# A tuned transformer kernel whose first two superblocks follow one written order for every engine

## The chip, the cores and the metric

The kernel runs on one core of one Trainium2 chip. The metric is device time in microseconds (us) of one execution. TensorE is called PE here (its weight loads are PEld), VectorE is DVE, ScalarE is ACT, GpSimd is POOL, and SyncE, which issues most of the DMAs, is SP. Each engine executes its own instruction queue strictly in order; engines wait for each other and for DMAs through semaphores.

## The reference

Sixteen sequences of 256 tokens with 256 features pass through a feed-forward block, an attention block and the same feed-forward block again, each with a layernorm in front and a residual around it:

```python
def _L0_ffn_ref(x, W_up, W_gate, W_down):
    def ternary_quant(w):
        scale = jnp.mean(jnp.abs(w)) + EPS          # EPS = 1e-8
        q = jnp.clip(jnp.round(w / scale), -1.0, 1.0) * scale
        return w + jax.lax.stop_gradient(q - w)
    wu, wg, wd = ternary_quant(W_up), ternary_quant(W_gate), ternary_quant(W_down)
    up = jnp.einsum('bsd,ed->bse', x, wu)            # 256 -> 1024
    gate = jnp.einsum('bsd,ed->bse', x, wg)
    hidden = jax.nn.silu(up) * gate
    return jnp.einsum('bse,de->bsd', hidden, wd)     # 1024 -> 256

x = x + 0.5 * _L0_ffn_ref(_layernorm(x), W_up, W_gate, W_down)
x = x + _L0_attn_ref(_layernorm(x), Wq, bq, Wk, bk, Wv, bv)   # 16 heads of 16, 4 key groups, causal
x = x + 0.5 * _L0_ffn_ref(_layernorm(x), W_up, W_gate, W_down)
```

A ternary weight is 0, +scale or -scale: it is not 0 where |w| > scale / 2, and it has the sign of w. The scale is a mean over the whole matrix, so no weight can be used before all of its matrix is loaded and summed.

## The kernel before

**Tiling.** The 4096 tokens are cut into 8 superblocks of 512 tokens (two sequences each). The work on superblock n in pass p (0 for the first feed-forward, 1 for the second) has the key (n, p). A superblock's input stays in a tile `x0` ... `x7`. Each feed-forward is 8 units f = 0 to 7. A unit makes `u` (up) and `g` (gate) by four 512-column matmuls each (two halves of the contraction, and a high and a low f16 part of the normalized input `xT`), then `th` = silu(u) on ACT, `h` = g * th on DVE, and `hT` = the high f16 part of h (a cast on ACT) and the low part (a subtraction on POOL). Four `ffn_down` steps (t = 0 to 3), of 16 matmuls of 256 columns each, make `d` from `hT` and the ternary weights `td`; DVE adds it to x.

**Start.** SP loads x0, the up weights in four pieces, the gate weights, x1, the down weights, the attention weights `wqkv` and the rest of x. The weights are summed (`part_u`, `part_g`, `part_d`), a matmul with ones spreads the sum over the partitions (`allsum_u` and so on), and `ternary_piece` makes the ternary f16 tiles `tu`, `tg`, `td` in pieces of 512 columns: first `dn` = (w < -scale/2), on DVE, ACT or POOL by a letter in `ENG_U`, `ENG_G`, `ENG_D`, then (w > scale/2) - dn on DVE (line 321). Some matmuls of ones with ones (`warm`) stand between the first steps.

**Norms.** x0 and x1 (names `first`, `second`) are normalized and then transposed by PE (`xt`, tile `xT`). Every later norm goes another way: bn_stats and bn_aggr on DVE, `rstd` on POOL (line 339), `shift` and two quarters of `xn` on DVE, two quarters on ACT, the high part of `xparts` on ACT (line 364), the low part on POOL (line 367), and a transposing DMA on SP (line 372) to `xT_f` (feed-forward) or `xT_a` (attention). The first attention projection of superblock n, tile `qkv` (line 525), needs `xT_a` of n, and the scaled attention weights `wparts` (DVE and POOL, lines 1026 and 1027).

**Attention.** After `qkv`, the parts of q and k go through DRAM (`kd`, `qd`) back into `Qs` and `ks`, with constant rows that POOL makes at the start (`constant_rows`, lines 243 to 253) and SP copies there. Tiles `s`, `tops`, `pparts`, `pt` find row maxima; `st`, `pT`, `o`, `oT`, `ot` are scores, exponentials, products with the values and their transposes.

**What sets the order.** A planner, `run`, pops steps from five chains (feed-forward units, loads, maxima, attention, projections) by written costs and lags, and issues their instructions. The scheduling layer under it then orders each engine's queue by its own estimate of times, unless a piece of code asks for its program order. So the order at the start comes from the planner's constants (`C1`, `C2`, `TD`, `DR`, `PM`, `LAG_NORM0` and so on) and from that layer.

```python
    for at, fn in (
        (16, constant_queries), (PM + 11, projections_split), (KM, constant_rows), (KV, constant_values), ...
        (C3, lambda: ternary_columns(3)), (C2, lambda: ternary_columns(2)), (C1, lambda: ternary_columns(1)),
    ):
        f.insert(at, Step(0.0, fn))
    run(f, [prepares(), load_chain(), sequence_chain(), peak_chain(), qkv_chain()])
```

Of the kernel before, what the change touches and what calls it, by code (L numbers as in the profile page):

```python
# [8 lines left out]
F32 = mybir.dt.float32  # L9
F16 = mybir.dt.float16  # L10
# [15 lines left out]
ENG_U = "vvvv"  # L26
ENG_G = "vapa"
ENG_D = "aaaa"
NUF = "000000"
NWF = "404000"  # L30
# [7 lines left out]
NCUT = 4  # L38
PINF = 0
NW4 = 0  # L40
PRE = 0
USUM = 1
GSUM = 0
PING = 0
HPU = 0
GFIRST = 0
PINF1 = 0
TDA = 1
PINK = 1
KM = 2  # L50
KV = 12
PINA = 0
PINM = 1
PINT = 0
NWARM = 12
NWARM2 = 0
NWARM3 = 0
GCUT = 0
# [9 lines left out]
C1 = 1  # L68
C2 = 4
C3 = 5  # L70
TD = 6
DR = 6
DS = 2
PM = 9
LAG_NORM0 = 10.0
DOWN_AT0 = 5
DOWN_GAP0 = 1
GU = 1
# [15 lines left out]
NORM = 1024.0  # L94


@with_exitstack
def macaron_kernel(
# [45 lines left out]

    x_t = x.rearrange("(n s) (t p) e -> n p (s t) e", s=2, t=2)
# [44 lines left out]
    load_x(0)  # L190
    for w, w_t in ((wu, w_upT), (wg, w_gateT)):
        for i in range(NCUT if w is wu or GCUT else 1):
            nn = NCUT if w is wu or GCUT else 1
            cut = slice(i * F // nn, (i + 1) * F // nn)
            nc.sync.dma_start(w[:, :, cut], w_t.rearrange("(c p) f -> p c f", p=P)[:, :, cut])
    load_x(1)
    nc.sync.dma_start(wd, w_downT.rearrange("(c p) e -> p c e", p=P))

    def load_rest():
        nc.sync.dma_start(wqkv, w_qkv.rearrange("(c p) f -> p c f", p=P))  # L200
        nc.sync.dma_start(bqkv, b_qkv)
        for n in range(2, NSB):
            load_x(n)
# [5 lines left out]
    nc.vector.tensor_copy(identh, ident)  # L209
    ones = const.tile([P, P], F32, tag="ones", name="ones")  # L210
    nc.vector.memset(ones, 1.0)
    neg_half = const.tile([P, TT], F32, tag="neg_half", name="neg_half")
    nc.vector.memset(neg_half, -0.5)

    def warm(n, name):
        if n:
            pw = bank([P, P], f"warm_{name}")
            for _ in range(n):
                nc.tensor.matmul(pw, ones, ones, start=True, stop=True)

    warm(NWARM, "start")

# [3 lines left out]

    box = {}
# [10 lines left out]
    def constant_rows():  # L238
# [4 lines left out]
        nc.gpsimd.memset(k[KP:KR], 0.0)  # L243
        ku = k[KP:KR].rearrange("p (v u k) -> p v u k", v=3, k=U)
        for which, base in ((EVEN, 0), (ODD, 32)):
            nc.gpsimd.affine_select(
                out=ku[:, which], in_=ku[:, which], pattern=[[0, S // U], [-1, U]],
                compare_op=ALU.is_ge, fill=-MASK, base=base, channel_multiplier=1,
            )
        nc.gpsimd.memset(k[KR : KR + 3], -MROW)  # L250
        nc.gpsimd.memset(v[KP:KR], 0.0)
        vj = v[KP:KR].rearrange("p (j b) -> p j b", b=4)
        nc.gpsimd.affine_select(
            out=vj, in_=vj, pattern=[[1, 32], [0, 4]], compare_op=ALU.not_equal,
            fill=MASK, base=0, channel_multiplier=-1,
        )
        for to in Ks:
            nc.sync.dma_start(
                to[KP : KR + 3].rearrange("p g v k -> p g (v k)"),
                k[KP : KR + 3].unsqueeze(1).to_broadcast([KR + 3 - KP, G, 3 * S]),  # L260
            )
        box["queries"] = v

    def constant_values():
        for v in VT:
            nc.gpsimd.memset(v, 0.0)
            nc.gpsimd.memset(v[:, :, :, D : D + 1], 1.0)
# [9 lines left out]
    def ternary_sums(w, name):  # L277
        if name == "d":
            cuts = [(w[:, : FC // 2], 1), (w[:, FC // 2 :], 1)]
        elif name == "u" or GCUT:  # L280
            fq = F // NCUT
            cuts = [(w[:, :, i * fq : (i + 1) * fq], 0 if i % 2 == 0 and not USUM else 1) for i in range(NCUT - 1)]
            h = fq // 2
            cuts += [(w[:, :, (NCUT - 1) * fq : (NCUT - 1) * fq + h], 0), (w[:, :, (NCUT - 1) * fq + h :], 1)]
        else:
            cuts = [(w[:, : EC // 2], GSUM), (w[:, EC // 2 :], 1)]
        part = small.tile([P, len(cuts)], F32, tag="part", name=f"part_{name}")
        for i, (piece, on_scalar) in enumerate(cuts):
            if on_scalar:
                junk = fp.tile([P] + list(piece.shape[1:]), F16, tag="th", name=f"junk_{name}_{i}")  # L290
                nc.scalar.activation(junk, piece, AF.Abs, accum_out=part[:, i : i + 1])
            else:
                pin(PING and name == "g", nc.vector.tensor_reduce(
                    part[:, i : i + 1], piece, AX.XY, ALU.add, apply_absolute_value=True
                ))
        return part

    def ternary_scale(w, name, part):
        n = w.shape[1] * w.shape[2]
        allsum = bank([P, part.shape[1]], f"allsum_{name}")  # L300
        nc.tensor.matmul(allsum, ones, part, start=True, stop=True)
        tot = small.tile([P, 1], F32, tag="tot", name=f"tot_{name}")
        nc.vector.tensor_reduce(tot, allsum, AX.X, ALU.add)
        s = const.tile([P, 1], F32, tag=f"s_{name}", name=f"s_{name}")
        nc.vector.tensor_scalar(s, tot, 1.0 / (P * n), TERNARY_EPS, ALU.mult, ALU.add)
        hi = small.tile([P, 1], F32, tag="hi", name=f"hi_{name}")
        nc.vector.tensor_scalar(hi, s, 0.5, None, ALU.mult)
        lo = small.tile([P, 1], F32, tag="lo", name=f"lo_{name}")
        nc.vector.tensor_scalar(lo, s, -0.5, None, ALU.mult)
        return s, hi, lo  # L310

    def ternary_piece(wi, ti, hi, lo, name):
        engine = {"u": ENG_U, "g": ENG_G, "d": ENG_D}[name[0]][int(name[1])]
        dn = fp.tile([P] + list(wi.shape[1:]), BF16, tag="tmp", name=f"dn_{name}")
        if engine == "a":
            nc.scalar.activation(dn, wi, AF.Relu, bias=lo, scale=-1.0)
            nc.scalar.activation(dn, dn, AF.Sign)
        else:
            by = nc.gpsimd if engine == "p" else nc.vector
            pin(PINT and engine == "v", by.tensor_scalar(dn, wi, lo, None, ALU.is_lt))  # L320
        nc.vector.scalar_tensor_tensor(ti, wi, hi, dn, ALU.is_gt, ALU.subtract)  # L321


    def norm_stages(n, name, factor, finish, early=False):
        xn = lnp.tile([P, TT, E], F32, tag="xn", name=f"xn_{name}", bufs=1)
        mv = small.tile([P, TT, nc.vector.BN_AGGR_DIM], F32, tag="mv", name=f"mv_{name}")
        rstd = small.tile([P, TT], F32, tag="rstd", name=f"rstd_{name}")

        def stats():
            st = small.tile([P, TT, nc.vector.BN_STATS_DIM], F32, tag="st", name=f"st_{name}")  # L330
            for t in range(TT):
                pin(PINA if name[0] == "a" else PINF1 if name in ("f0_1", "f0_2") else PINF if name[:2] == "f0" else 0, nc.vector.bn_stats(st[:, t, :], xs[n][:, t, :]))
            for t in range(TT):
                nc.vector.bn_aggr(mv[:, t, :], st[:, t, :])
            ve = small.tile([P, TT], F32, tag="ve", name=f"ve_{name}")
            nc.vector.tensor_scalar(
                ve, mv[:, :, 1], LN_EPS, 1.0 / (factor * factor), ALU.add, ALU.mult
            )
            nc.gpsimd.tensor_tensor(rstd, ve, neg_half, ALU.pow)

        def normalize():
            on_scalar = 2 if name in ("first", "second") else NACT0 if early else NACT
            shift = small.tile([P, TT], F32, tag="shift", name=f"shift_{name}")
            nc.vector.scalar_tensor_tensor(shift, mv[:, :, 0], -1.0, rstd, ALU.mult, ALU.mult)
            for t in range(TT):
                if t < on_scalar:
                    nc.scalar.activation(
                        xn[:, t, :], xs[n][:, t, :], AF.Identity,
                        bias=shift[:, t : t + 1], scale=rstd[:, t : t + 1],
                    )  # L350
                else:
                    nc.vector.tensor_scalar(  # L352
                        xn[:, t, :], xs[n][:, t, :], mv[:, t, 0:1], rstd[:, t : t + 1],
                        ALU.subtract, ALU.mult,
                    )

        return [stats, normalize] + [lambda f=f: f(xn) for f in finish]

    def ffn_norm(n, name, tag="xT", early=False):
        parts = lnp.tile([P, 2, EC, TT, P], F16, tag="xparts", name=f"xparts_{name}")  # L360
        xT = lnp.tile([P, 2 * EC * TT, P], F16, tag=tag, name=f"xT_{name}", bufs=2 if tag == "xT" else 1)

        def high(xn):
            nc.scalar.copy(parts[:, 0].rearrange("p c t e -> p t c e"), xn.rearrange("p t (c e) -> p t c e", c=EC))  # L364

        def low(xn):
            nc.gpsimd.tensor_tensor(  # L367
# [3 lines left out]
            )  # L371
            nc.sync.dma_start(xT, parts.rearrange("p a c t e -> p (a c t e)"), transpose=True)

        view = xT.rearrange("p (a c t) q -> p a c (t q)", a=2, c=EC)
        return view, norm_stages(n, name, NORM, [high, low], early)

    def early_norm(n, name):
# [724 lines left out]
```

## Time and profile before

| | |
|---|---|
| median of 3 runs | 563.08 us (561.78 to 563.2) |
| the profiled execution | 560.4 us; its span 558.7 us |
| PE busy | 537.8 us, 96% of the span |
| DVE, ACT, POOL busy | 433.1, 376.0, 355.0 us (78%, 67%, 64%) |
| TensorE clock granted, mean | 0.991 |

The busy share of PE is an average over stages; matmuls overlap in a pipeline, and a busy PE may run at half clock. The views used below give, for each group of instructions, the start and the duration in us, the engine, the line of the kernel, the operation, the tiles written and read, and in brackets how long that engine had been idle just before and what ended the idleness. SPq is a DMA's issue on SP. In the windows view, a time and a count of instructions stand for each engine, then the granted clock and the DMA engines' share.

### The profile page before, as it was taken

Reading aid. Unit: us, or ns where it says so; the run is one execution under the profiler, and the core shown is the slowest. Engines: PE = TensorE matmul, PEld = TensorE weight load, DVE = VectorE, ACT = ScalarE, POOL = GpSimd, SP = SyncE. Lnnn points to the kernel's source line nnn. Section 1 sums busy time; section 2 is a strip of 40 time slices with the busy share of each in tenths; the row PEclk is TensorE's granted clock in tenths of the full one; section 3 lists DMA queues with packets and bytes.
Section 4 is the critical chain, followed back from the end, with each engine's and each line's share of the span. In section 5 each row is a group of like instructions: output and inputs, shape, how many; then the busy total and the mean of one; then the engine's idle time right before and its main releaser. Section 6 shows DMA issues by size and latency. Waiting matters only on the chain.

```text
span 558.7 us, 12132 instructions
## 1 busy us (share of the span) xinstructions
PE 537.8 (96%) x4593; PEld 330.6 (59%) x4593; DVE 433.1 (78%) x1027; ACT 376.0 (67%) x658; POOL 355.0 (64%) x380
## 2 busy tenths in 40 slices
PE   5999999989999999999999998999999999999997
PEld 5546556647556665665665664566645576565565
DVE  5988989978889899869777887459955697847653
ACT  5796757496688678677766749755698445874642
POOL 4367787675589568577745539854589534865542
PEclk8899999999999999999999999999999999999999
DMA  8933288561077068058249003572024930020201
GB/s 293 299 48 57 39 207 128 161 124 31 12 185 111 1 163 144 4 152 147 27 126 163 1 3 39 144 162 40 1 40 74 207 79 22 12 68 11 67 28 49
DMA packets 119317, 51.25 MB, mean 92 GB/s; under 512 B 85174, under 2 KB 119002, under 8 KB 119258
## 3 DMA queue, kind: packets, MB, share of 16 engines
q1 hardware_dynamic: 118825, 50.08, 40.8%
q8 instruction: 36, 0.59, 0.4%
q10 hardware_dynamic: 432, 0.39, 0.3%
q14 instruction: 24, 0.19, 0.1%
HBM read 22.41 MB, written 14.68 MB: 66 GB/s over the span
## 4 chain that ended last, share of the span: by engine, by line
PE 72%; DVE 11%; ACT 7%; DMA 5%; POOL 3%; issue 2%; SPq 0%; DVEq 0%; ACTq 0%; POOLq 0%
PE d L502 18%; PE u L451 15%; PE g L451 15%; PE o L706 6%; PE s L611 6%; PE st L675 5%; PE qkv L525 4%; DMA Qs<-prows 2%; ACT pT L676 2%; PE ot L722 2%; DVE tops L625 2%; DVE h L486 1%; DVE tmp L485 1%; DMA xT_a<-xparts_a 1%; DVE xn_f L352 1%
## 5 line engine op out<-in xcount | busy, mean ns | idle before, releaser
L492 POOL TENSOR_TENSOR hT<-h,hT 128x512 f16<-128x512 f32 x128 | 149.0, 1169 | 88.0 <-ACT hT L491 87.1
L676 ACT ACTIVATE pT<-st,exp_scale 128x512 f32<-128x512 f32 x192 | 119.8, 697 | 26.3 <-PE st L675 26.2
L502 PE MATMUL d<-td,hT 128*128 128x256 f16 x1024 | 122.5, 273 | 0.2 <-ACT pT L676 0.2
L491 ACT CAST hT<-h 128x512 f16<-128x512 f32 x128 | 79.5, 621 | 56.0 <-DVE h L486 40.9
L625 DVE TENSOR_REDUCE tops<-s 128x8 f32<-128x512 f32 x160 | 103.0, 677 | 16.3 <-PE s L611 15.9
L451 PE MATMUL u<-xT_f,tu 128*128 128x512 f16 x448 | 115.3, 379 | 0.3 <-DVE h L486 0.3
L684 POOL TENSOR_SCALAR_AFFINE_SELECT pT<-pT 128x512 f32<-128x512 f32 x128 | 80.4, 636 | 55.3 <-ACT pT L676 52.9
L451 PE MATMUL g<-xT_f,tg 128*128 128x512 f16 x448 | 115.3, 379 | 0.0
L502 PEld LDWEIGHTS <-hT 128*128 128x128 f16 x1024 | 98.5, 98 | 18.2 <-issue 0.5
L485 DVE SCALAR_TENSOR_TENSOR tmp<-th,u 128x512 f32<-128x512 f32 x96 | 65.5, 683 | 50.4 <-ACT th L483 49.9
L483 ACT ACTIVATE th<-u,half_u 128x512 f32<-128x512 f32 x96 | 66.2, 692 | 42.8 <-PE u L451 42.4
L451 PEld LDWEIGHTS <-tg 128*128 128x128 f16 x512 | 49.9, 98 | 62.0 <-DVE tg L321 2.0
L451 PEld LDWEIGHTS <-tu 128*128 128x128 f16 x512 | 47.2, 99 | 43.1 <-issue 2.0
L486 DVE SCALAR_TENSOR_TENSOR h<-g,tmp 128x512 f32<-128x512 f32 x96 | 65.6, 685 | 5.4
L675 PE MATMUL st<-Qs,ks 99*128 99x512 f16 x192 | 54.1, 380 | 6.3 <-DMA Qs<-prows 3.0
L611 PEld LDWEIGHTS <-Qs 96*128 96x128 f16 x896 | 50.9, 116 | 12.7 <-issue 3.0
L611 PE MATMUL s<-ks,Qs 96*128 96x64 f16 (+2 forms) x896 | 53.4, 208 | 0.0
L706 PE MATMUL o<-pT,vt 128*32 128x128 f32 (+1 forms) x1024 | 49.4, 329 | 0.0
L706 PEld LDWEIGHTS o<-pT,vt 128*32 128x32 f32 x1024 | 28.4, 109 | 25.2 <-issue 8.3
L507 DVE SCALAR_TENSOR_TENSOR x<-d,so,x 128x256 f32<-128x256 f32 x64 | 30.4, 477 | 14.1 <-PE d L502 13.6
L525 PE MATMUL qkv<-xT_a,wparts 128*128 128x512 f16 x144 | 34.6, 379 | 1.9 <-DMA xT_a<-xparts_a 1.9
L367 POOL TENSOR_TENSOR xparts_f<-xn_f,xparts_f 128x1024 f16<-128x1024 f32 x14 | 29.8, 2131 | 10.2 <-ACT xparts_f L364 8.2
(163 smaller groups left out, 603.2 us busy)
## 6 DMA issues: line engine op xcount, KB each, us to landing
qd<-sp SPq DMA_DIRECT2D x32, 256.0 KB, 2.6
Qs<-qd SPq DMA_DIRECT2D x64, 128.0 KB, 3.5
ks<-kd SPq DMA_DIRECT2D x48, 128.0 KB, 3.6
x<-in_x SPq DMA_DIRECT2D x8, 512.0 KB, 8.7
out<-x SPq DMA_DIRECT2D x32, 128.0 KB, 3.1
kd<-sp SPq DMA_DIRECT2D x16, 128.0 KB, 2.4
Qs<-in_w_upT SPq DMA_DIRECT2D x4, 256.0 KB, 5.5
Qs<-in_w_gateT SPq DMA_DIRECT2D x1, 1024.0 KB
```

The source lines that it names most:

```text
L451: nc.tensor.matmul(acc, w[:, c, f * P : (f + 1) * P], ffn_ready[key][:, a, c, :], start=(c == 0 and a == 0), stop=(c == EC - 1 and a == 1),)
L485: nc.vector.scalar_tensor_tensor(tmp, th, 1.0, up, ALU.add, ALU.mult)
L486: nc.vector.scalar_tensor_tensor(h, gate, 0.25 / (NORM * NORM), tmp, ALU.mult, ALU.mult)
L491: nc.scalar.copy(hT[:, f, 0, :], h)
L492: nc.gpsimd.tensor_tensor(hT[:, f, 1, :], h, hT[:, f, 0, :], ALU.subtract)
L502: nc.tensor.matmul(acc, hT[:, f, a, t * P : (t + 1) * P], td[:, f, :], start=(f == 0 and a == 0), stop=(f == FC - 1 and a == 1),)
L611: nc.tensor.matmul(sc[:, at : at + n, :], Qs[0:KR, b // 4, g * P : (g + 1) * P, b % 4], k[:, g, which, first * U : (first + n) * U], start ...
L625: nc.vector.tensor_reduce(peaks[q][:, u, :], sc, AX.X, ALU.max)
L675: nc.tensor.matmul(sc, keys, mov, start=True, stop=True)
L676: nc.scalar.activation(pT[:, u, :].rearrange("p (h b j) -> p h b j", h=4, b=4), sc.rearrange("p (h j b) -> p h b j", h=4, b=4), AF.Exp, sc ...
L684: nc.gpsimd.affine_select(out=v, in_=v, pattern=[[0, 4], [1, P]], compare_op=ALU.is_ge, fill=0.0, base=0, channel_multiplier=-1,)
L706: pin(not first, nc.tensor.matmul(at[:, half * P :], v[:, 2 * s + half, g, :], moving, start=half == 0, stop=half == 1, tile_position=(0, ...
```

## The change

Everything up to the end of superblock (0, 0)'s `ffn_down` and of superblock (1, 0)'s units is taken from the planner and written as one table, `ORDER`, of 191 words; each word issues one small step. Calls go through a wrapper that keeps the program order on each engine while the table is read (`box["in_order"]`). After the table, the planner goes on with superblock (2, 0), with attention, and with the four `ffn_down` of (1, 0); the scheduling layer orders that part as before.

- **Ternary weights:** ACT stores |w| (`sizes`, f32) while it sums it; `sign` = (w >= 0) - 0.5 is made on POOL (`:P`, 8 of 12 pieces of 512 columns) or DVE (`:V`); then one DVE step makes (|w| > cut) * sign. The values are now halves, and the scales carry the factor 2. The sums of up and gate are made in three parts: two on ACT, one of 512 columns on DVE. For the down weights ACT writes |w| in place.
- **Loads:** x0 in two halves by token tiles, up and gate in two halves by rows each, all at the head of SP's queue.
- **Warm matmuls:** 14 at the start, 12 after `all_u`, 4 after `all_g` (before: 12, and two times 4 between the first products).
- **Norms of x0 and x1:** x0 by halves and on DVE alone; x1 as before.
- **Constants of attention:** POOL's memsets of `vt` and its `constant_rows` stand after the table; SP's copies `ks<-constant_rows` follow the first `xT_a` on SP's queue, and the copies `Qs<-constant_rows` stand among the loads of the first two sequences.
- **Planner:** the two table superblocks count as done, and superblock 2's norm as ready.

```diff
-NWARM = 12
+NWARM = 14
+ORDER = """
+st0 ag0 st1 rs0 ag1 xn0 rs1 su0 tr0 xn1 su1 gu1:P su1v tr1 azu gu0:V allu warm12 gu2:V hi00 oneu
+cutu hi01 peru gu3:P tu0a sg0 tu1 sg1v sg1 lo00 gg2:P azg tu0b allg warm4 s1a lo01 gg0:P tu2 U02 tu3
+U04 th02 s1b gg1:P U01 misc th04 agg1 gd3:V U06 th01 cutg gg3:V rs1x tg0b U00 tg0a tg3 G00 gd2:P sh1
+...
+alld U14 th10 cutd miscd td0 H11 U13 rs2 th14 td2 U17 L11 th13 xV2 U16 sh2 h14 xA2 td1 G10 H14 td3
+G17 ph2 L14 h10 D3 th17 pl2 th16 h17 H10 D1 r3 H17 L10 END2 D2 r1 L17 G13 r2 G15 h13 U15 H13 L13 D0
+th15 h15 G16 H15 r0 L15 h16 H16 L16
+"""
...
-    load_x(0)
+    for s in range(2):
+        nc.sync.dma_start(xs[0][:, 2 * s : 2 * s + 2], x_t[0][:, 2 * s : 2 * s + 2])
     for w, w_t in ((wu, w_upT), (wg, w_gateT)):
-        for i in range(NCUT if w is wu or GCUT else 1):
...
+        for c in range(EC):
+            nc.sync.dma_start(w[:, c], w_t[c * P : (c + 1) * P])
...
-        if engine == "a":
-            nc.scalar.activation(dn, wi, AF.Relu, bias=lo, scale=-1.0)
-            nc.scalar.activation(dn, dn, AF.Sign)
-        else:
-            by = nc.gpsimd if engine == "p" else nc.vector
-            pin(PINT and engine == "v", by.tensor_scalar(dn, wi, lo, None, ALU.is_lt))
-        nc.vector.scalar_tensor_tensor(ti, wi, hi, dn, ALU.is_gt, ALU.subtract)
...
+    def size_pass(n, c, lo, hi, i=None):
+        scalar.activation(
+            size[n][:, c, lo:hi], raws[n][:, c, lo:hi], AF.Abs,
+            **({} if i is None else {"accum_out": part[n][:, i : i + 1]}),
+        )
+    def half_sign(engine, n, cut):
+        engine.tensor_scalar(sign[n][cut], raws[n][cut], 0.0, 0.5, ALU.is_ge, ALU.subtract)
+    def ternary(n, cut):
+        src = size[n] if n in size else raws[n]
+        vector.scalar_tensor_tensor(tern[n][cut], src[cut], cuts[n], sign[n][cut], ALU.is_gt, ALU.mult)
...
+    for name in ORDER.split():
+        if name[:4] == "warm":
+            warm(int(name[4:]))
+            continue
+        name, _, engine = name.partition(":")
+        ops[name](*([by[engine]] if engine else []))
+    constant_values()
+    constant_rows()
+    box["in_order"] = False
+    vector.tensor_copy(identh, ident)
+    constant_keys()
...
+    for t in range(TT):
+        issued["down", 0, 0, t] = 0.0
     f = ffn_chain()
-    for at, fn in (
-        (16, constant_queries), (PM + 11, projections_split), (KM, constant_rows), (KV, constant_values), ...
+    for at, fn in ((C_QUERIES, constant_queries), (C_SPLIT, projections_split), (C_TOP, projections_top)):
         f.insert(at, Step(0.0, fn))
```

In the table, U, G, th, h, H, L with two digits are superblock and unit (u, g, silu, join, high, low), D0 to D3 and r0 to r3 are the matmuls and the residual of (0, 0)'s `ffn_down`, g with a letter and a digit is a sign piece and t with them a ternary piece.

The changed kernel, as built, has these orders around the end of the table. PE: D3, D1, D2, then three products, D0, G16, then u and g of (2, 0)'s units 0 to 4 with three `ffn_down` of (1, 0) among them, then `qkv` of superblock 0. DVE after r0's residual: one bn_stats of x0, four of x3, `h`, a small step, five bn_aggr, `h`, a small step, then the variance step of x0. POOL after L16: a `vt` memset, `rstd` of x0, `rstd` of x3, three `hT` low parts with four more memsets among them, the low part of `wparts`, the low part of `xparts_a` of superblock 0. ACT, for the same norm: silu, the first two scalings of `wqkv`, `xn` of x0, the third scaling, an `hT` cast, then the high part of `xparts_a`. SP, after qkv of superblock 0: the transposing DMA of `xT_a` of superblock 1 stands behind 23 DMAs for attention of superblock 0, three of which are the copies `Qs<-constant_rows` (20 DMAs stand there before the change, without these copies).

## The prediction

> **What bounds the kernel now.** I read the page first: PE's busy share and the clock by slices.
>
> ```profile
> PE 537.8 (96%) x4593; PEld 330.6 (59%) x4593; DVE 433.1 (78%) x1027; ACT 376.0 (67%) x658; POOL 355.0 (64%) x380
> ...
> PEclk8899999999999999999999999999999999999999
> ```
>
> PE sets the pace, except in the first slices, where the clock is low too. A gain here must be PE time not lost. So next PE's own timeline of the start, then the granted clock in windows.
>
> ```profile
> 13.69 0.56 PE L301 MATMUL allsum_g<-part_g,ones 128*128 128x2 f32 x2 [0.69 <-ACT xT_first L388]
> 14.11 0.59 PE L451 MATMUL u<-xT_first,tu 128*128 128x512 f16 x1
> ...
> 18.35 1.38 PE L451 MATMUL g<-xT_first,tg 128*128 128x512 f16 x4 [0.67 <-DVE tg L321]
> ...
> 23.49 0.82 PE L451 MATMUL g<-xT_first,tg 128*128 128x512 f16 x3 [0.28 <-DVE tg L321]
> ```
>
> ```profile
> 5.43:8.84 3.41, 0.66 (x6) 0.47 (x5) 1.41 (x9) 2.33 (x7) 1.91 (x3) 1.00 1.01 372
> 8.84:19.08 10.24, 7.35 (x26) 4.90 (x27) 9.37 (x38) 5.62 (x11) 1.01 (x1) 0.50 1.08 353
> ```
>
> DVE is busy 9.37 of 10.24 us; its ternary pieces release PE. PE runs at half clock from 8.84 to 19.08, after 2.75 us of idleness out of 3.41. By 23.49 it has done five groups of four products. A group takes 0.86 us at full clock (the chain of waits steps by 0.86), so PE stands as if it had begun at 23.49 - 5 x 0.86 = 19.2 and never stopped. From there to 43 us it hardly waits.
>
> The table ends near 50 us. So I also read the timeline of the other engines across the first attention norm:
>
> ```profile
> 51.32 0.45 DVE L507 SCALAR_TENSOR_TENSOR x<-d,so,x 128x256 f32<-128x256 f32 x1
> ...
> 52.73 1.01 POOL L339 TENSOR_TENSOR rstd_a<-ve_a,neg_half 128x4 f32<-128x4 f32 x1 [2.90 <-DVE ve_f L336]
> ...
> 54.52 1.08 ACT L347 ACTIVATE xn_a<-x,shift_a,rstd_a 128x256 f32<-128x256 f32 x2
> ...
> 58.50 2.13 POOL L367 TENSOR_TENSOR xparts_a<-xn_a,xparts_a 128x1024 f16<-128x1024 f32 x1
> ...
> 60.66 1.85 SPq L372 DMA_TRANSPOSE xT_a<-xparts_a  x1
> ```
>
> It is 9.3 us from the last residual of superblock 0 to the issue of its transposing DMA. The page gives 4.6 us from issue to landing for xT_f and 5.7 for xT_a. The first qkv starts at 66.27, 5.6 us after the issue, without an idle PE: there is little to spare.
>
> **The start: -4.6 us.** I walk the built queues with these durations. I keep the landing of the weights: ACT reads up's last piece at 8.67 and gate at 11.31. (If longer rows land sooner, the walk gains up to 0.7 us.)
>
> - ACT: two sums of gate are now 1.14 us for 1024 columns and 0.73 for 512 (from the same pass over the old pieces, with the read of the accumulator), so all_g is fed at 12.5, not 13.69.
> - DVE per 512 columns: the last ternary step keeps its 0.66 us start to start. The sign costs the 0.40 of the old dn on 4 pieces and nothing on 8. The sum of a 512-column part is 0.6, against 1.21 for the old gate half.
> - ACT loses the Relu and Sign passes (0.7 + 0.6 us on six pieces) and gains |w| passes of 0.54; it is not late in the walk.
> - POOL: eight sign pieces at 1.73 (the one row, dn_g at 19.78). They end two to four us ahead of their users.
> - 4 warm matmuls (0.21 each at full clock) hide until the last low part of xT; first product at 14.2, fifth group done at 18.9, none waiting more than 0.25 us after that.
>
> So PE stands as if it had begun at 18.9 - 5 x 0.86 = 14.6, against 19.2: -4.6 us.
>
> **POOL's new work: +1.0 (0 to +7).** The dn_g row had no second two-input DVE step on top of it. The hT low parts at 27.48 to 32.7 took 5.26 us for 4, or 1.32, against 1.17 in the page's mean, while DVE made td and tg pieces. If sign pieces took 2.3 us the walk's gate products wait 2.4 us; at 3.0 us, 7. Below nothing is excluded: POOL is early already. I take 1.0, nearer the 1.73 row. The Trainium skill ("SBUF — State Buffer", "SBUF: two separate sides") speaks against this edit: a DVE step with both inputs in SBUF and a GpSimd step that reads SBUF exclude each other for the whole step. Both new steps are of that kind. By that rule alone each sign piece may wait out one 0.75 us ternary step, 2.4 us apiece, and the term would be nearer 2.5.
>
> **The clock: +1.0 (0 to +5).** The row above shows half clock for 10.24 us after 2.75 us idle. The longer warm-up covers the start, but the stall below is 5.5 us idle. Half of 10.24 is 5.1; a dense PE should have it back sooner, and part of it falls into the second stall. The Trainium skill ("TensorE: Matmul & The Clock Gate", "What's actually happening") says one idle window of about 3.4 us halves the clock, and one busy window restores it. By that rule it costs 1.7 us per stall.
>
> **The end of the table: +5.5 (0 to +6.7).** PE, from 18.9: 27 groups of the table (23.3), 8 transposes (0.9), the sum of down (0.4), four downs of 1.75 (7.0), then a transpose and a small matmul (0.4), 10 groups (8.6) and three downs of superblock 1 (5.2): it reaches qkv at 64.7. Now the data:
>
> - D0 ends at 49.5; residual at 49.7. DVE then has five bn_stats (1.7), two h (1.3), five bn_aggr (0.4) and two small steps (0.4) before the variance: 53.9. Before, that step came 1.2 us after the residual; now 4.2.
> - POOL is in L16 until 54.5, then a vt memset (0.46), rstd (1.0): 55.9. DVE's shift and xn: 56.8.
> - ACT has two scalings of wqkv first, which wait for DVE's reciprocal chain (57.0): 57.5 to 58.4. Then xn (1.0), a scaling, a cast, the high part (1.0): 61.2. Before, xn came 0.6 us after shift.
> - POOL has two hT parts, memsets, a third hT part and wparts (2.07, behind DVE's cast at 60.3) first: 63.5. Low part 2.1: 65.6. SP issues at 65.7; landing 4.5 later, 70.2; by the 5.7, 71.4.
>
> PE waits from 64.7 to 70.2. Nothing stands behind qkv in PE's queue that could run: the queue is in order. Before, the same path is 9.3 us; here it is 16, and only 15 us of PE work lie over it after D0.
>
> **The second norm: +3.7 (0 to +4).** From qkv to the next superblock's qkv PE has 20 us of work (5.2 for qkv and values, 14 of products and downs, 0.5 of s): it arrives at 90.2. In before, from the end of that superblock's last down (77.6) to the DMA's issue (87.6) is 10.0 us. Here that down ends at 77.7, the low part at 87.5, and SP reaches the DMA only at 89.4, because three Qs<-constant_rows copies of 0.63 each now stand before it. Landing 93.9.
>
> **The rest: +1.7 (-2 to +5).** The planner goes on from other counts. In before's waits of PE after 110 us: st on prows 3.0, st on pT 2.0, qkv on xT_a 1.9, pt on pparts 1.3, together 8.2. Walking the new queues I find pt (1.7, 2.7), qkv (2.2), st (1.5, 1.8): 9.9. +1.7.
>
> The POOL constants cost nothing on PE otherwise: ks is needed by s 20 us later. The warm matmuls lie in idle time.
>
> **Sum.** -4.6 + 1.0 + 1.0 + 5.5 + 3.7 + 1.7 = +8.3. From the profiled 560.4: 568.7. The median of the runs, 563.08, is 0.5% above that execution; scaled, 571.
>
> **Rivals.**
>
> 1. *Faster:* the first norm's data is there in time. If xT_a of superblock 0 is issued before about 60 us, neither the first wait nor the clock loss exists, and the second shrinks with it: -4.6 + 1.0 + 0.7 = -2.9, or 560. For it: before has no wait there, and the table puts PE early but the norm's chain as early. Against: three queues have been given extra steps ahead of that chain (DVE 3 us, ACT 2, POOL 4). Chance 0.22.
> 2. *The POOL pieces bound the start:* 2.3 to 3.0 us each, gate products waiting; the waits at the table's end stay, since everything moves along: 571 + 1.4 to 6, that is 573 to 577. For it: the 1.32 row; against: POOL's slack of 2 us. Chance 0.18.
> 3. *About nothing:* start and waits cancel; needs the first wait at 2 us and the second at 1. Chance 0.06.
> 4. The forecast, 565 to 573: 0.54.
>
> That the table does not do what it says I leave out: the built queues follow it.
>
> **How the numbers follow.** 0.3% of 563 is 1.7 us, about what a measurement of this kernel can tell from no change. Faster: rival 1. Within: rival 3. Slower: 0.18 + 0.54 = 0.72. The range: 559.5 takes in rival 1's own time and cuts what lies below it (half of its chance), and 577 cuts the top of the POOL bound with a late xT_a.
>
> **What would show it.** PE's first product near 14.2 and the fifth group done near 19; POOL's sign pieces at 1.7 (rival 2: over 2.3, with PE waiting for tg between 18 and 30). PE dense to about 64, then idle 4 to 7 us before qkv, ended by DMA xT_a, and once more, 3 to 4 us, near 90. A PE that runs through both would make the prediction wrong; so would a first product after 17.

## The result, and the profile after

The changed kernel takes 585.26 us (median of 4 runs, 585.13 to 586.83) against 562.46 for the kernel before (the three runs above and one more): the ratio is 1.0421, with a 95% interval of 1.0395 to 1.0448. The forecast was slower, 571; the time is 14 us above it and outside the range of 559.5 to 577.

The page of the changed kernel, PE's busy share, the granted clock by slices, and the group of the attention projections:

```profile
PE 545.2 (93%) x4623; PEld 335.4 (57%) x4623; DVE 443.7 (76%) x1025; ACT 371.0 (64%) x644; POOL 370.2 (63%) x388
...
PEclk9999989599999999899999999999999999999999
...
L139 PE MATMUL qkv<-xT_a,wparts 128*128 128x512 f16 x144 | 38.3, 410 | 18.7 <-DMA xT_a<-xparts_a 18.7
```

All wrapped calls carry the wrapper's line, L139, so one goes by tiles. The slices no longer show a low clock at the start (the windows view still has 0.61 from 10.97 to 15.35), but the eighth slice (102 to 117 us) stands at half clock, and PE waited 18.7 us for `xT_a`. PE's timeline shows where (first three lines: the start, where each f32 matmul shows as two instructions, so x24 are twelve warm matmuls; then both waits):

```profile
10.97 4.55 PE L139 MATMUL warm<-ones 128*128 128x128 f32 x24
15.35 0.74 PE L139 MATMUL all_g<-part_g,ones 128*128 128x1 f32 x6
...
16.92 4.48 PE L139 MATMUL u<-xT_first,tu 128*128 128x512 f16 x20
...
73.96 5.43 PE L139 MATMUL qkv<-xT_a,wparts 128*128 128x512 f16 x18 [5.29 <-DMA xT_a<-xparts_a]
...
97.80 0.64 PE L139 MATMUL s<-ks,Qs 96*128 96x192 f16 x10 [1.61 <-issue]
108.82 2.74 PE L139 MATMUL qkv<-xT_a,wparts 128*128 128x512 f16 x6 [10.37 <-DMA xT_a<-xparts_a]
```

The last `d` before the first wait ends at 68.67 (66.76 plus 1.91). The first product comes at 16.9, not 14.2.

**A ledger of the loss.** Take a matmul's start and subtract the full-speed time of all matmuls ahead of it (the median start-to-start time of each form in all runs). The warm matmuls and those that sum the weights are not counted, since the two kernels have different numbers of them. What is left is the time that PE has lost so far. Read at equal amounts of work, the two profiled executions compare like this:

| PE work done | lost before | lost, changed | difference | what lies in the step |
|---|---|---|---|---|
| 30 us | 18.8 | 16.7 | -2.1 | the start |
| 50 us | 18.9 | 17.8 | -1.1 | `every` waits 0.94 for DVE: +1.0 |
| 60 us | 19.0 | 24.7 | +5.7 | first wait, 5.3, and half clock: +6.8 |
| 70 us | 18.9 | 25.4 | +6.5 | `d` waits 0.55 for `hT`: +0.8 |
| 80 us | 19.2 | 40.5 | +21.3 | second wait, 1.6 + 10.4, and half clock: +14.8 |
| 470 us | 79.3 | 104.2 | +24.9 | the rest: +3.6 |

The spans differ by the same 24.9 (583.6 against 558.7). Three fifths of the loss is the second wait with its half clock. SP's timeline from qkv of superblock 0 to `xT_a` of superblock 1 shows why; first the kernel before (two of its lines), then the changed one:

```profile
69.78 2.21 SPq L372 DMA_TRANSPOSE xT_f<-xparts_f  x1
...
87.61 2.82 SPq L372 DMA_TRANSPOSE xT_a<-xparts_a  x1
```

```profile
74.41 3.15 SPq L249 DMA_DIRECT2D ks<-constant_rows  x3
77.68 5.56 SPq L336 DMA_TRANSPOSE xT_f<-xparts_f  x1
83.33 1.40 SPq L603 DMA_DIRECT2D kd<-sp  x2
84.78 0.65 SPq L261 DMA_DIRECT2D Qs<-constant_rows  x1
...
92.50 6.95 SPq L626 DMA_DIRECT2D Qs<-qd  x8
99.49 0.63 SPq L632 DMA_DIRECT2D ks<-kd  x1
100.16 1.36 SPq L261 DMA_DIRECT2D Qs<-constant_rows  x2
101.63 5.35 SPq L336 DMA_TRANSPOSE xT_a<-xparts_a  x1
```

The second column is how long SP was held by the issue. Behind three `ks` copies the transposing DMA holds SP for 5.56 us instead of 2.21, and everything for attention stands behind it. `xparts_a` of superblock 1 is ready at 96.2 (POOL 94.08 plus 2.14); SP gets to it at 101.63, and its data release PE at 108.8, 7.2 us after the issue. The windows view after the first wait, then around the end of the second (the last three figures are the granted clock, the DMA engines' share and GB/s):

```profile
74.00:76.00 2.00, 2.00 (x5) 0.65 (x5) 0.00 (x0) 0.03 (x1) 1.86 (x3) 0.50 0.00 0
76.00:78.00 2.00, 2.00 (x9) 0.84 (x8) 0.47 (x1) 0.78 (x1) 1.36 (x2) 0.80 0.42 131
...
104.00:108.80 4.80, 0.00 (x0) 0.00 (x0) 0.00 (x0) 0.00 (x0) 0.00 (x0) 0.50 1.14 177
108.80:112.00 3.20, 3.18 (x13) 1.52 (x14) 0.00 (x0) 1.44 (x2) 1.95 (x1) 0.50 0.72 133
112.00:114.50 2.50, 2.50 (x11) 1.08 (x10) 2.00 (x3) 0.38 (x1) 0.57 (x2) 0.53 0.00 0
```

From 104 to 108.8 no engine works and the DMA engines are full. Half clock then costs 1.4 us after the first wait (2 us at 0.50, 2 at 0.80) and 2.8 after the second.

### The profile page after: what moved, and what is told of

Its sections match the earlier page's. It is cut to its first block, busy times and chain, and to the rows that moved or that the text cites. A ratio compares the mean times of both kernels' runs of the same rounds, so it can differ in the third digit from the quotient of the medians.

```text
span 583.6 us, 12183 instructions
## 1 busy us (share of the span) xinstructions
PE 545.2 (93%) x4623; PEld 335.4 (57%) x4623; DVE 443.7 (76%) x1025; ACT 371.0 (64%) x644; POOL 370.2 (63%) x388
## 4 chain that ended last, share of the span: by engine, by line
PE 64%; DVE 14%; DMA 7%; ACT 6%; POOL 5%; issue 2%; SPq 0%; ACTq 0%; DVEq 0%; POOLq 0%
PE d L139 15%; PE u L139 12%; PE g L139 11%; PE o L139 6%; PE s L139 5%; PE qkv L139 5%; PE st L139 5%; DVE h L139 3%; DMA xT_a<-xparts_a 3%; DVE tmp L139 2%; DVE tops L139 2%; PE ot L139 2%; POOL hT L139 2%; ACT pT L139 2%; ACT th L139 2%
## 5 line engine op out<-in xcount | busy, mean ns | idle before, releaser
L139 POOL TENSOR_TENSOR hT<-h,hT 128x512 f16<-128x512 f32 x128 | 149.0, 1169 | 85.3 <-ACT hT L139 84.9
L139 ACT ACTIVATE pT<-st,exp_scale 128x512 f32<-128x512 f32 x192 | 120.6, 694 | 26.0 <-PE st L139 25.8
L139 DVE TENSOR_REDUCE tops<-s 128x8 f32<-128x512 f32 x160 | 103.4, 680 | 27.1 <-PE s L139 27.0
L139 PE MATMUL d<-td,hT 128*128 128x256 f16 x1024 | 122.5, 273 | 0.5 <-POOL hT L139 0.5
L139 ACT CAST hT<-h 128x512 f16<-128x512 f32 x128 | 79.4, 621 | 63.6 <-DVE h L139 63.4
L139 PE MATMUL u<-xT_f,tu 128*128 128x512 f16 x448 | 116.3, 381 | 0.4
L139 POOL TENSOR_SCALAR_AFFINE_SELECT pT<-pT 128x512 f32<-128x512 f32 x128 | 81.0, 637 | 55.8 <-ACT pT L139 55.3
L139 PE MATMUL g<-xT_f,tg 128*128 128x512 f16 x448 | 115.1, 379 | 0.0
L139 PEld LDWEIGHTS <-hT 128*128 128x128 f16 x1024 | 98.9, 98 | 20.4 <-POOL hT L139 0.8
L139 ACT ACTIVATE th<-u,half_u 128x512 f32<-128x512 f32 x96 | 66.1, 690 | 42.2 <-PE u L139 41.4
L139 DVE SCALAR_TENSOR_TENSOR tmp<-th,u 128x512 f32<-128x512 f32 x96 | 65.4, 682 | 35.8 <-ACT th L139 35.2
L139 PEld LDWEIGHTS <-tg 128*128 128x128 f16 x512 | 50.2, 98 | 59.8 <-issue 0.8
L139 PEld LDWEIGHTS <-tu 128*128 128x128 f16 x512 | 47.0, 99 | 44.1 <-issue 2.1
L139 DVE SCALAR_TENSOR_TENSOR h<-g,tmp 128x512 f32<-128x512 f32 x96 | 65.9, 687 | 6.3
L139 PEld LDWEIGHTS <-Qs 96*128 96x128 f16 x896 | 50.7, 117 | 16.8 <-issue 5.8
L139 PE MATMUL s<-ks,Qs 96*128 96x64 f16 (+2 forms) x896 | 53.4, 209 | 3.4 <-issue 1.6
L139 PE MATMUL st<-Qs,ks 99*128 99x512 f16 x192 | 54.0, 380 | 2.4 <-DMA Qs<-prows 1.1
L139 PE MATMUL qkv<-xT_a,wparts 128*128 128x512 f16 x144 | 38.3, 410 | 18.7 <-DMA xT_a<-xparts_a 18.7
L139 PE MATMUL o<-pT,vt 128*32 128x128 f32 (+1 forms) x1024 | 49.1, 329 | 0.2 <-DVE tops L139 0.2
L139 DVE SCALAR_TENSOR_TENSOR x<-d,out_scale,x 128x256 f32<-128x256 f32 x64 | 30.5, 479 | 22.6 <-PE d L139 22.0
L139 POOL TENSOR_TENSOR sp<-full,sp 128x512 f16<-128x512 f32 (+1 forms) x24 | 28.0, 1166 | 22.9 <-DVE sp L139 19.2
L139 PEld LDWEIGHTS o<-pT,vt 128*32 128x32 f32 x1024 | 28.4, 109 | 24.5 <-issue 7.5
```

Of the source, the lines that this page charges most:

```text
L139: ins = fn(*args, **kwargs)
```

## The experiments

The theories are four. A: the constants of attention, late on POOL, SP and the DMA queue, make the waits. B: the norm's own chain on DVE, ACT and POOL is late whatever SP does. C: POOL's work between L16 and `xparts_a` makes the first wait. D, for the start: the loads by halves land late, and idle PE costs the clock (the expectation of experiment 4 has its own letter A for the loads). Time lost always means the ledger. Ratios are to the runs of the kernel before beside them.

**1. The constants not pinned.**

```diff
-    constant_values()
-    constant_rows()
     box["in_order"] = False
+    constant_values()
+    constant_rows()
```

> The changed kernel with one line moved: the program order is switched off before POOL's constants are issued (vt and constant_rows), not after, so the scheduling layer may put them early, and SP's six copies of constant_rows with them, ahead of xT_f of superblock 2. Theory A (the constants late on POOL, SP and the DMA queue make the waits for xT_a): the second wait of PE for xT_a, 12.0 us with the wait before it, falls to 0 to 4, the first, 5.3, to 1 to 5, and the half clock behind them (about 3.5 us) goes with them: 585 falls to 566 to 572. Theory B (the norm's own chain on DVE, ACT and POOL is late, whatever SP does): the first wait stays above 4 and the second above 8, time 579 or more. The start stays as it is in both: first product at 16.9.

580.56 us, ratio 1.0328 (1.0286 to 1.0369). A's number missed; B's number fits, but not its waits. The layer put `xparts_a` ahead of the third `hT` part, and the first wait shrank to 1.2 (for `wparts`) and 1.6 (at `v`). But POOL's `constant_rows` (2.10 us) now lay ahead of `rstd_second`, for which DVE and then PE's `g` waited 0.93 each (18.4 lost at 20 us of work, against 16.4). And the second wait was still 6.3, though no copies of constants stood on SP's queue there any more: PE came to it at 94.1, and `xT_a` was issued at 95.59. So moving these instructions early is not enough by itself: where they go decides, and without the copies the norm of superblock 1 is still late for a PE that comes early.

**2. Only the copies and their source early.**

```diff
-... rs1 su0 tr0 xn1 ...
+... rs1 krow su0 tr0 xn1 ...             # krow: constant_rows, on POOL
     constant_values()                    # the vt memsets stay behind L16
-    constant_rows()
     box["in_order"] = False
     constant_keys()
+    constant_queries()                   # no longer at step C_QUERIES
```

> The changed kernel with constant_rows made at the start of POOL's queue (in the table, behind the second rstd of x0) and SP's six copies issued before xT_f of superblock 2; the vt memsets stay pinned behind L16. Theory A split: if SP and the DMA queue make the second wait, it falls from 12 us to under 3, while the first wait, in which only POOL's memsets could matter, stays at 4 to 6: 571 to 575. If the memsets on POOL make both, the second wait stays over 6: 578 or more. Theory B: 583 or more.

572.29 us, ratio 1.0179 (1.013 to 1.0227). PE's timeline and waits of this run, then SP's two transposing DMAs:

```profile
99.33 1.47 PE L139 MATMUL qkv<-xT_a,wparts 128*128 128x512 f16 x6 [1.08 <-DMA xT_a<-xparts_a]
```

```profile
PE qkv L139 <- DMA xT_a<-xparts_a: 9.3, 3, 5.2
```

```profile
74.90 1.70 SPq L336 DMA_TRANSPOSE xT_f<-xparts_f  x1
...
94.16 3.17 SPq L336 DMA_TRANSPOSE xT_a<-xparts_a  x1
```

The columns of the second, for the whole run, are us in total, times, and the longest. The first wait is 5.2 as before; the second is 1.08, and 26.1 are lost at 80 us of work against 40.5. SP reached `xT_f` at 74.90 for 1.70 us, and `xT_a` at 94.16 instead of 101.63. PE got its data at 99.33, 9.5 us sooner: `xparts_a` was ready 3.2 us earlier (93.0), SP took 1.2 us instead of 5.4 to get to it, and the landing 5.2 instead of 7.2. This shows A for the second wait, worth 13 us of time, and shows that the copies have no part in the first. POOL's steps for `constant_rows` (3.0 us between 69.63 and 77.44 in the changed kernel) moved together with SP's copies, so the experiment does not tell the two apart.

**3. The other way round: the kernel before with its constants late.**

```diff
-KM = 2
+KM = 26                                  # constant_rows; each POOL call pinned
-        (16, constant_queries), ...
+        (32, constant_queries), ...
```

> The kernel before with only its constants late: the memsets of constant_rows are pinned in program order on POOL and issued at step 26 of the feed-forward chain, the copies to Qs at step 32, so that SP's six copies stand between the transfers of the first attention, ahead of xT_a of superblock 1, as in the changed kernel. Theory A: the kernel before gets a wait of 4 to 12 us between 75 and 100 us, at s or at qkv, and half clock behind it: 563 rises to 569 to 577. Theory B: the old norm chain has room, and it stays below 566.

577.47 us, ratio 1.0281 (1.0226 to 1.0336). PE and SP of this run:

```profile
96.53 1.04 PE L611 MATMUL s<-ks,Qs 96*128 96x192 f16 x10 [11.09 <-DMA Qs<-constant_rows]
```

```profile
91.86 2.97 SPq L271 DMA_DIRECT2D Qs<-constant_rows  x3
94.93 6.08 SPq L372 DMA_TRANSPOSE xT_a<-xparts_a  x1
```

This alone costs the kernel before 15 us, with 32.5 lost at 80 us of work against 19.2. The wait is at `s`, for the copies themselves, so it is the same cause by another path; and again a transposing DMA right behind three copies holds SP for 6.08 us.

**4. The loads of before.**

```diff
-    for s in range(2):
-        nc.sync.dma_start(xs[0][:, 2 * s : 2 * s + 2], x_t[0][:, 2 * s : 2 * s + 2])
+    load_x(0)
...
-        for c in range(EC):
-            nc.sync.dma_start(w[:, c], w_t[c * P : (c + 1) * P])
+        nn = 4 if w is wu else 1            # up in 4 pieces of columns, gate whole
...
```

> The changed kernel with the loads of before: x0 whole, the up weights in four pieces of columns, the gate weights whole. In the changed kernel the two halves of up were waited for until 8.44 and 9.7 us, in before the last piece until 8.6. Theory A (halves by rows land later and so cost the start about 1 us): the sums of up are done about 1 us sooner, PE idles less before the warm matmuls, the first product comes at 15.4 to 16.2 instead of 16.9, and the time falls by 0.7 to 1.5 us. Rival (the norm of x0 or the sums of gate set the start): first product within 0.4 us of 16.9 and the time within 0.5 us.

586.23 us, ratio 1.0462 (1.0399 to 1.0524); the start as PE shows it:

```profile
10.46 2.92 PE L139 MATMUL warm<-ones 128*128 128x128 f32 x24
13.22 0.73 PE L139 MATMUL all_g<-part_g,ones 128*128 128x1 f32 x6
13.81 1.14 PE L139 MATMUL warm<-ones 128*128 128x128 f32 x8
14.79 4.75 PE L139 MATMUL u<-xT_first,tu 128*128 128x512 f16 x20
```

In this execution D seems to hold: ACT reads up from 8.18, the first product comes at 14.79, the same warm matmuls take 2.92 instead of 4.55 at a granted clock of 1.00 instead of 0.61 (window 10.97 to 15.35), and 1.4 us less are lost at 30 us of work (15.3). But the time did not fall: the advantage was 3 us at 120 us of work, 1.7 at 320, and gone at 380. And the later runs show that 8.18 was a lucky landing: up in four pieces was there only at 9.0, 9.2, 9.0 (experiments 7, 8, 13), 8.6 and 9.2 (the kernel before and experiment 14). The two halves came at 8.0 to 8.4 and 9.3 to 9.7 in six executions. So, going by these landings, the loads are worth about half a microsecond, within a scatter of 1, and one profile was not enough to tell.

**5. The vt memsets early too.** Experiment 2, and:

```diff
-st0 ag0 st1 ...
+vals st0 ag0 st1 ...                     # vals: constant_values
```

> The second experiment (copies early) with the six vt memsets also moved, from behind L16 to the head of POOL's queue. There PE still waited 5.2 us for xT_a of superblock 0, and POOL's queue between L16 and xparts_a held five vt memsets (1.6 us) and three hT low parts. Theory C (what POOL does between L16 and xparts_a makes the first wait): with the memsets gone the layer also puts xparts_a ahead of the third hT part and wparts; the wait falls to 0.5 to 2, the half clock behind it goes, and the time falls by 4 to 6 from that experiment's 572, to 566 to 568. Rival (ACT's scalings of wqkv or DVE's statistics are what comes last): the wait stays over 4 and the time within 2 us of 572.

574.78 us, ratio 1.0234 (1.0196 to 1.0273). C was half right. The first wait for `xT_a` is gone (1.2 for `wparts` and 1.55 at `v` remain; 20.5 lost at 60 us of work instead of 24.8). But nothing was gained: PE came earlier to the second qkv and waited there, as its timeline shows:

```profile
98.07 2.47 PE L139 MATMUL qkv<-xT_a,wparts 128*128 128x512 f16 x6 [3.74 <-DMA xT_a<-xparts_a]
```

At 80 us of work 26.5 are lost, against 26.1 in experiment 2. The landing of the second `xT_a`, not PE's arrival, set the time.

**6. The first qkv later in PE's queue.** Experiment 5, and:

```diff
-LAG_NORM0 = 10.0
+LAG_NORM0 = 16.0
```

> The fifth experiment (all constants early) with LAG_NORM0 16 instead of 10, so that the first qkv stands later in PE's queue, behind more products of superblock 2. Theory: what is left of the two waits for xT_a (1 to 2 us each) goes to zero and nothing new comes by 130 us, so 2 to 4 us less than the fifth. Rival: SP and the DMA queue are the limit and the wait moves to u of superblock 3 or to s, behind xT_f or Qs: same time as the fifth within 1.5.

566.5 us, ratio 1.0096 (1.0059 to 1.0133): 8 us less than experiment 5, since both waits for `xT_a` are gone. A new one came, which neither theory had put at this size:

```profile
82.21 0.69 PE L139 MATMUL v<-ident,full 64*128 64x64 f32 x4 [3.22 <-ACT full L139]
```

`full` stands behind the norm of superblock 1 in ACT's queue. With half clock behind it (0.80 on average from 84 to 88 us), 22.2 are lost at 70 us of work, 3.3 more than in the kernel before.

**7 and 8. Old loads on top, then two lags of the planner.** Experiment 6 with the loads of experiment 4 and LAG_NORM0 15; and with LAG_NORM0 16, LAG_ROWS 6 (was 4), LAG_MAX 6 (was 5).

> All constants early, LAG_NORM0 15, and the loads of before (up in four pieces, x0 and gate whole). With the old loads the changed kernel's first product came at 14.8 instead of 16.9, but its time did not fall, since a later wait took it back. Theory: without the waits for xT_a the start's gain of 1.4 to 2 us stays, and the time is that much under the sixth's, 560 to 563. Rival: the later waits (pt, st, qkv after 300 us) take it back again: within 0.5 of the sixth.

> As the seventh with LAG_NORM0 16, and two of the planner's lags longer: LAG_ROWS 6 instead of 4 and LAG_MAX 6 instead of 5, which put pt and the exponents later in PE's queue. In the changed kernel PE waits 5.0 us for pparts at pt and 2.2 at st. Theory: these waits fall by 4 to 7 us and the time to 554 to 558, under both kernels. Rival: later exponents push the last attention towards the end and the tail eats it: 560 or more.

569.27 us, ratio 1.0142 (1.0104 to 1.0179), and 564.35 us, ratio 1.0049 (1.0011 to 1.0088). Both missed. The old loads now made the start worse, not better: first product at 18.4 and 17.4, 18.3 and 18.1 lost at 30 us of work. Up was there 0.8 to 1 us later than in experiment 4, and the clock was 0.50 and 0.61 from 10.97 to 15.35. Experiment 8 takes 4.9 us less than 7, but LAG_NORM0 differs as well, and 2.0 of the difference stand in the ledger by 80 us of work (23.7 lost against 25.7); what the two lags do alone is tested in experiment 14.

**9 and 10. The start alone.** Experiment 6 with `tr0 warm4 xn1`, `tr1 warm4`, `allu warm8` in the table; and experiment 6 with up in four pieces, gate whole, x0 still in halves.

> The sixth experiment (constants early, later qkv) with the warm matmuls of the start placed otherwise: four behind the first transposes of x0, four behind the second, eight instead of twelve behind all_u. In the sixth, PE idled between 8 and 10.5 us, the granted clock was 0.67 from 10.97 to 15.35, and the twelve warm matmuls took over 4 us instead of 2.6. Theory (idle PE halves the clock, and the twelve then hold all_g up): PE idles less, the clock stays at 1.00 in that window, and the first product comes at 14.8 to 15.8 instead of 16.9; time 1 to 2 us less than the sixth. Rival (the sums of gate and the low part of xT set the first product, not PE): it comes at 16.3 or later, time within 0.7.

> The sixth experiment with up loaded in four pieces of columns and gate whole, as before; x0 stays in halves. In the fourth experiment old loads brought the first product to 14.8, in the seventh and eighth, with x0 whole and POOL's constants ahead of rstd, to 17.4 to 18.4. Theory: the last piece of up is there near 8.7 instead of 9.7, so all_u and the warm matmuls begin 0.7 to 1 us sooner and PE does not idle long enough to lose its clock: first product 14.8 to 15.8, time 1 to 2 us less than the sixth. Rival: POOL's constants delay rstd and xn whatever the weights do: first product 16.5 or later, same time.

567.99 us, ratio 1.0101 (1.0064 to 1.0138), and 568.38 us, ratio 1.0123 (1.0096 to 1.015). In 9 the clock stayed at 1.00 and the first product came at 15.3, as expected, but then:

```profile
15.32 0.81 PE L139 MATMUL u<-xT_first,tu 128*128 128x512 f16 x3
16.39 0.38 PE L139 MATMUL u<-xT_first,tu 128*128 128x512 f16 x1 [0.25 <-DVE xT_first L139]
17.29 2.98 PE L139 MATMUL u<-xT_first,tu 128*128 128x512 f16 x13 [0.53 <-DVE tu L139]
```

PE runs into DVE's pieces, and 16.9 are lost at 30 us of work, not less than the 16.7 of experiment 6: DVE is the next bound right behind. That the warm matmuls keep the clock is not shown: experiment 5, without them, had 1.00 in the same window too (first product at 15.24), and experiment 12, with them, had 0.61. The window in 9, then in 12:

```profile
10.97:15.35 4.38, 3.83 (x31) 3.46 (x31) 4.05 (x12) 2.93 (x7) 4.38 (x3) 1.00 1.08 356
```

```profile
10.97:15.35 4.38, 4.37 (x25) 4.37 (x25) 3.79 (x11) 3.61 (x8) 4.38 (x3) 0.61 1.09 355
```

In 10 all of up was there only at 9.7; PE waited 2.1 us for its sums and the clock fell to 0.61.

**11 and 12. Together.** Both edits of 9 and 10, with LAG_ROWS and LAG_MAX 6; 11 with LAG_NORM0 13 and the lag of `v` 5 for superblock 0, 12 with LAG_NORM0 16.

> Both edits of the start, LAG_NORM0 13, the lag of v 5 instead of 2 for superblock 0, LAG_ROWS and LAG_MAX 6. In the sixth PE waited 3.2 us at v for ACT's full, which ACT's queue held behind the norm of superblock 1. Theory: with the qkv a little earlier and v later that wait falls under 1.5, and a wait for xT_a of up to 1.5 stays; with the longer lags the time is 554 to 558. Rival: v and xT_a wait as before, 560 or more.

> The eighth experiment (later qkv, lags of 6) with the start of the ninth and tenth together instead of the old loads. Theory: the start's 1.5 to 3 us (first product at 17.4 there) are all kept, 561.5 to 563 where the eighth had 564. The wait at v of 3.2 us stays. Rival: a later wait eats it, 564 or more.

568.63 us, ratio 1.0109 (1.0066 to 1.0152), and 562.88 us, ratio 1.0013 (0.9982 to 1.0043). 11 missed by 10 us: the wait at `v` went and one of 4.7 us for the second `xT_a` came. Between `v` and `xT_a` one can choose, with this norm chain. 12 is level with the kernel before, with the wait at `v` of 3.2 in it. Its time lies in the range that was expected, but not for the reason given: its start gained little (first product at 16.5, 16.9 lost at 30 us of work).

**13 and 14. What was open: POOL at the start, and whose gain the lags are.** 13 is experiment 8 with `vals krow` at the head of the table (`krow` no longer behind `rs1`). 14 is the kernel before with two constants:

```diff
-LAG_ROWS = 4.0
+LAG_ROWS = 6.0
-LAG_MAX = 5.0
+LAG_MAX = 6.0
```

> The eighth experiment (old loads, all constants early, LAG_NORM0 16, lags of 6) with constant_rows moved on from behind x0's second rstd to the head of POOL's queue, behind the vt memsets. Theory (there POOL's constants cost the start 2 us by delaying rstd and the first sign pieces): the first product comes at 14.8 to 15.5 as in the fourth experiment, not at 17.4, the clock stays full, and the time falls by 1.5 to 2.5 from the 562.9 of the twelfth, to 560 to 561.5. Rival (with x0 whole the start is decided by the weights' landing): first product at 16.5 or later, 562.5 or more.

> The kernel before with nothing but LAG_ROWS 6 instead of 4 and LAG_MAX 6 instead of 5. In it PE waits 3.0 us at st for prows, 2.0 at st for pT and 1.3 at pt for pparts. Theory (these lags are worth the same to both kernels and have nothing to do with the change): those waits go and the time falls by 3 to 6, to 555 to 558, under every version of the changed kernel so far. Rival (the lags mend an order that only the changed kernel has): within 1.5 us of 561.

13: 562.9 us, ratio 1.0005 (0.998 to 1.003), above the 560 to 561.5 expected. The first product came at 15.6, just outside what was expected; the clock stayed at 1.00, and 16.4 were lost at 30 us of work, against 18.1 in 8. Of the 1.8 us between the two first products, 1.6 are the twelve warm matmuls, 2.92 us instead of 4.55 by the clock. Experiments 5 and 6 differ as much (2.92 and 4.45 us, clocks of 1.00 and 0.67) with the same table, so this does not show that POOL's order did it; and the median did not follow.

14: 555.49 us, ratio 0.9876 (0.9858 to 0.9893): 1.2% faster than the kernel before, and as expected. PE's waits in the kernel before, then in this run:

```profile
PE st L675 <- DMA Qs<-prows: 3.0, 4, 1.1
...
PE qkv L525 <- DMA xT_a<-xparts_a: 1.9, 1, 1.9
PE pt L654 <- DVE pparts L646: 1.3, 1, 1.3
```

```profile
PE st L675 <- DMA Qs<-prows: 0.9, 1, 0.9
```

The wait for `prows` falls from 3.0 to 0.9, and those at `pt` and for `xT_a` are no longer among the listed ones. The gain of these lags belongs to the planner and not to the change; with the same lags, the repaired changed kernel (13) is still 7 us behind.

## Why the prediction was wrong, step by step

The side and the places were right. The sum was +8.3 and the ledger has +24.9; half of what is missing is one step.

- **The second norm (+3.7, 0 to +4): 12.0 us of waiting (1.6 at `s` and 10.4 at `qkv`), and 2.8 of half clock behind it, which the sum has under another term. This is the step that failed.** It counted the three `Qs<-constant_rows` copies at 0.63 of SP's time each and let the DMA land 4.5 us after its issue. Without the wait at `s` PE would have come to this `qkv` at 96.8, and the missing 8.3 us are three pieces: `xparts_a` was ready 0.6 us before that and not 2.7; SP got to its DMA 5.4 us later and not 1.9; the landing took 7.2 and not 4.5. The copies also hold the transposing DMAs behind them: 5.56 and 5.35 us of SP instead of 2.21 and 2.82, 6.08 in experiment 3. The three `ks` copies, and `xT_f` with its waiting issue, stood ahead of `kd`, which delayed the whole path of attention (`kd` was issued 9.4 us after the first `qkv` began, 4.4 in experiment 2), and the step put them at nothing. The sentence that POOL's constants cost PE nothing otherwise was wrong for the same reason. Experiment 2 shows it by moving the constants out of the way, 13 us, and experiment 3 by moving those of the old kernel into it, 15 us. In both POOL's steps move with SP's copies; how much of the loss is POOL's stays open.
- **The end of the table (+5.5): 5.3 us of wait**, as walked; both ends of it came 4 us late together (PE at 68.7 instead of 64.7, the data at 74.0 instead of 70.2). What comes last there was named as a queue of steps on three engines. Experiment 5 shows that the memsets on POOL, and the order that the layer makes with them, are enough to explain it, and also that removing the wait pays nothing while the second stands.
- **The start (-4.6) and POOL's pieces (+1.0): together -2.1 in the ledger**, where the sum has -3.6; by the prediction's own measure the start is -2.3 (16.9 against 19.2). Three things were mis-sized. The landing of up was kept at 8.67, with "up to 0.7" to gain; the last half was there at 9.73. The twelve warm matmuls took 4.55 us at a clock of 0.61, after PE's idle 1.5 and 0.5 us; the walk had them at full clock, where they take 2.92 (experiment 4). And with both out of the way DVE's pieces wait next (experiment 9), where the walk saw no wait over 0.25. The best start seen, experiment 4's with an early landing and full clock, is -3.5, about what the walk had. POOL's sign pieces took 1.9 to 2.25 us, between the row's 1.73 and the 2.4 estimated from the rule of the Trainium skill ("SBUF — State Buffer", "SBUF: two separate sides"); the rows do not tell how long they waited for DVE. PE's waits in the changed kernel show none for `tg`, so no wait shows this term, and rival 2 fell.
- **The clock (+1.0, 0 to +5): 1.4 after the first wait and 2.8 after the second.** The range held it; the value did not: it had part of the half clock fall into the second stall, and each wait brought its own. An estimate by the rule of the Trainium skill ("TensorE: Matmul & The Clock Gate", "What's actually happening") is 1.7 for each wait: near the first, too little for the second, where 0.50 lasted to about 114.
- **The rest (+1.7, -2 to +5): +3.6**, inside. With 1.0 at `every` and 0.8 at `d`, which the sum did not have, all adds up to the 24.9 of the ledger.
- **Rival 1** (data there in time) needed `xT_a` issued before 60; it was issued at 69.54.

Left open: why up lands up to 1 us earlier or later with the same loads; why the clock from 10.97 to 15.35 is full in some executions and not in others; and whether a pinned order of ACT's `full` would free the 3.2 us at `v`, which was not tried.

## What to carry to other kernels

An instruction that nobody waits for soon is not free when it is pinned behind other work: ask what its DMAs stand in front of in the issuing queue, and how long that queue is held by the next DMA behind them, not only by their own issue. When two waits stand in one chain, removing the first can pay nothing (experiment 5); count them together. Before crediting a large reordering, try the few constants of the planner that it leaves alone: here two lags in the old kernel gave 7 us, more than any version of the new order.

## What the runs showed of the hardware that was not expected

- A transposing DMA issued right behind two or three copies of constant rows (210 or 256 KB each) held SP for 5.35 to 6.08 us, in five places of three kernels; elsewhere around the first attention it took 1.4 to 3.4.
- In the first 10 us, the same four loads of up were all there between 8.2 and 9.2 us after x0 whole, in seven executions, so a start tuned to a microsecond is tuned to one of them.
- With one and the same table the granted clock from 10.97 to 15.35 was 1.00 in experiments 9 and 11 and 0.61 in experiment 12, where PE had not been idle for more than 0.70 us at a time since 6.3 us.
